# Weights of 1 and three second-read tiles in the batch-norm sums, and edge codes in 16 transfers, in a ragged-attention kernel

## The chip, the cores and the metric

The kernel runs on one core of one Trainium2 chip. The time is device microseconds of one execution. The time before is 331.27 us, the median of 4 runs from 331.06 to 331.68. A separate profiled execution gave the trace; its own time was 331.13 us, of which 326.7 us are the span of the profile.

## The reference

16384 rows of 256 features belong to 8 segments by `bids`, whose values come unsorted. Each row is to be found by its segment and its position (its number less the segment's start, which a binary search on the unsorted ids gives), so that several rows can fall on one place: one of them owns the place, the others lose it and read back the owner's row. Places before 0 or from LMAX on are at the segment's edges. Inside each segment there is softmax attention of all owners with each other, then a linear map, a batch norm over all 16384 rows, a relu and the residual.

```python
q = feat @ Wq                      # 256 -> 32, k likewise; v = feat @ Wv, 256 -> 256
starts = jnp.searchsorted(bids, jnp.arange(B, dtype=bids.dtype))
pos = jnp.arange(N, dtype=bids.dtype) - starts[bids]
qp, kp, vp = (pad(q), pad(k), pad(v))            # (8, 3072, .) by (bids, pos)
attn = jax.nn.softmax(masked qp kp^T, axis=-1)
r = (attn @ vp)[bids, pos]
t = r @ Wt
tn = (t - t.mean(axis=0)) / jnp.sqrt(t.var(axis=0) + EPS) * gamma + beta
return feat + jax.nn.relu(tn)
```

What matters here is the mean and the variance of `t`: sums over all 16384 rows of `t` and of its square, although `t` is computed only for the owners. An owner's row stands in the sums as often as it is read.

## The kernel before, in words

**Tiles.** The owners of a segment fill up to 6 tiles of 128 rows (`FT`), the rows that lost their place up to 3 more tiles for the whole kernel (`LT`); most other rows of the input read an edge row of one of the segments. The list of a segment's rows (`list_ahead`, L1147, `list_rows`, L1167) is made by VectorE (DVE) and TensorE (PE); GpSimd (POOL) then gathers the rows into `xs`. PE transposes them, projects q and k, and computes scores; ScalarE (ACT) takes exponents (`pa`, `pb`); `attend` (L1265) multiplies with the values, where the weights `Wv` and `Wt` are already joined, so that `scale` (L1278) has rows of `t` in `tk`. SyncE (SP) stores these to `t_rows` in DRAM.

**The sums.** For each tile of owners `square` (L1292) squares the rows on ACT, and `moments` (L1316) adds them and their squares to `acc` by two `scalar_tensor_tensor` on DVE, each row weighted by `reads_r`, the number of times it is read. `gather_reads` (L1191) fetches `reads_r` from DRAM, a tile of 128 weights at a time: 48 indirect gathers on POOL's queue. It is called in segments 1 to 6, where `list_part` and the slots of side work stand in the same hand-written order. `past(e)` (L1667) takes a few squares and moments from the lists `lag` and `squared`, so that they stay behind the attention by some steps.

**The order of the work.** The eight segments are one unrolled loop; in segment e the steps of `attend` are interleaved with the list, the gathers and the projection of later ones. The order in the source is the order of each engine's queue; semaphore waits are added from the tiles that instructions read and write. `slot()` puts in one or more pieces of side work (`work`): places of the losers, counts at the edges (`side_count`, which makes `below` and `above` from `pos`), `fill_rows` (L1633: clears `acc`, `xl`, `tl`, `ecat` and `reads_r`), and `part` (L1492).

**Edge codes.** Rows that read an edge row get it by a one-hot matmul in the last stage. `edge_of` in DRAM holds a code for each such row; `part` copies it into `eb` by 64 transfers on SP's queue, each to 16 partitions (L1503), and DVE compares it with the partition's own code and writes `hot`. In segment 1 POOL sets both `eb` buffers to 99 first (L1697), since the transfers leave 64 of the 128 partitions unwritten.

**The last segment** (L1714 on) takes its steps in the order 0, 1, 4, 5, 2, 3. SP starts ten loads of 1 MB of `feat` there. POOL computes `sel`, the selection of the edge rows, in six operations, and gathers the edge rows of the first seven segments into `ecat` (L1726). PE adds the last segment's, DVE joins them, ACT squares, and PE sums `ecat` weighted by `we` and `acc` into `sums`. Then come two 32x32 transposes, `scale`, `shift` and `y3`, the finished edge rows. After that a loop over 16 groups of 1024 rows adds `hot` times `y3` to the input rows (PE, then DVE's add into `f`), finishes the owners (`normal`, L1879, `normal_more`, both DVE), stores the groups (SP), and POOL scatters the owners (L1972) and the losers (L1985). The losers' rows, `tl`, are gathered from `t_rows` by the list `ridl` after the last segment (L1826). Ahead of the last segment come `slot(99)` and the memset of `none` on POOL (L1816, L1817).

Most operations are recorded by helpers, whose lines the profile shows: L802 matmul, L807 transpose, L812 activation, L817 and L818 copies on ACT and DVE, L821 tensor_tensor, L830 tensor_scalar (`ts`), L841 scalar_tensor_tensor, L854 reciprocal, L857 transposes on DVE, L860 memset, L877 gather, L893 scatter.

Of the kernel before, what the change touches and what calls it, by code (L numbers as in the profile page):

```python
# [14 lines left out]
AF = mybir.ActivationFunctionType  # L15
ALU = mybir.AluOpType
# [4 lines left out]
P = 128  # L21
NB = 8
# [6 lines left out]
FT = 6  # L29
FW = FT * P  # L30
LT = 3
# [869 lines left out]
def fast_path(nc, feat, bids, wq, wk, wv, wt, gamma, beta, out, bad):  # L901
    N, D = feat.shape
# [5 lines left out]
    NG = J // GT  # L908
    NL = NB + 1
    TT = NB * FT  # L910
    QA, QB = 4 * P, 2 * P
    pg = Fast(nc)

    room = ExitStack()
    start = nc._sbuf_addr_for_side("left")
# [23 lines left out]
    tk = new("tk", [P, TT, D])  # L939
# [126 lines left out]
    regs = pg.sized  # L1066

    def load(eng, key, ap, hi, lo=0):
        def emit(e):
            regs[key] = e.value_load(ap, min_val=lo, max_val=hi)  # L1070

        pg.op(eng, emit, [ap], [], bare=True)
# [36 lines left out]
    pg.tt(sm[:], sm[:], sc_[:], ALU.subtract, eng="POOL")  # L1109
    pg.tt(sm[:], sm[:], sa[:], ALU.add, eng="POOL")  # L1110

    def zero_fill(e):
        rows = xs[:, e * FT : (e + 1) * FT, :].rearrange("p t d -> p (t d)")
        pg.copy("ACT", rows, zero[:].to_broadcast([P, FT * D]))
# [32 lines left out]
    def list_ahead(e):  # L1147
        T = FT if e < NB else LT
        pg.ts(ge[:, 0, 0 : T * P], it16[:, 0 : T * P], cbeg[:, e : e + 1], ALU.is_ge)
        pg.ts(ge[:, 1, 0 : T * P], it16[:, 0 : T * P], cend[:, e : e + 1], ALU.is_ge, -1.0, ALU.mult)  # L1150
        pg.ts(pad[:, 0:T], rcol[:, 0:T], n_bc[:, e : e + 1], ALU.is_ge, float(N), ALU.mult)
        if e < NB:
            m = slice(e * FT, e * FT + T)
            pg.ts(mask[:, m], rcol[:, 0:T], n_1[:, e : e + 1], ALU.is_ge, NEG, ALU.mult)

    def list_sums(e, h, ps=None):
        ps = nb() if ps is None else ps
# [33 lines left out]
    def gather_reads(e):  # L1191
        for t in range(FT):
            m = e * FT + t
            pg.gather(reads_r[:, m : m + 1], reads_of, idx[:, m : m + 1], N)
# [95 lines left out]
    squared = []  # L1290

    def square(e, u):  # L1292
        n = e * FT + u
        x = sq[turn[1] % (4 if e < NB - 1 else 3)]
        turn[1] += 1
        pg.act(x[:], tk[:, n, :], AF.Square)
        return n, x
    def own_of(e):
        pg.ts(own1[:], b_f[:], float(e), ALU.is_equal)
        pg.stt(own1[:], tok[:], st_lo[:, e : e + 1], own1[:], ALU.is_ge, ALU.mult)  # L1300
# [13 lines left out]

    pg.copy("POOL", bs_f[:], bs_i[:])
    def moments():  # L1316
        m, s = squared.pop(0)
        x = m - TT + FT - 2
        one = rw[:, x : x + 1] if x in (0, 1) else reads_r[:, m : m + 1]
        pg.stt(acc[:, 0, :], tk[:, m, :], one, acc[:, 0, :], ALU.mult, ALU.add)  # L1320
        pg.stt(acc[:, 1, :], s[:], one, acc[:, 1, :], ALU.mult, ALU.add)

    cast_bids()
    pg.ts(own0[:], b_f[:], 0.0, ALU.is_equal, pm[:], ALU.mult)
# [80 lines left out]
    def slot(n=1):  # L1405
        for _ in range(n):
            if work:
                work.pop(0)()
# [34 lines left out]
    def edges():  # L1443
# [48 lines left out]
        def part(c):  # L1492
            x = eb[c % 2]

            def go():
                for k in range(C):
                    for r in range(4):
                        dst = x[32 * r : 32 * r + 2 * NB, k * W : (k + 1) * W]

                        def emit(e, c=c, k=k, r=r, dst=dst):  # L1500
                            g = regs[("order", C * c + k)]
                            src = edge_of[ds(g * W + r * NG * W, W)]
                            return e.dma_start(dst, src.unsqueeze(0).to_broadcast([2 * NB, W]))  # L1503

                        pg.op("SP", emit, [edge_of], [dst], dma=True)

            def end():
                pg.ts(
                    hot[:, C * c : C * c + C, :, :],
                    x[:].rearrange("e (k p u) -> e k u p", k=C, u=2), emod[:], ALU.is_equal,  # L1510
                )

            return go, end
# [114 lines left out]
    def fill_rows():  # L1628
        def zeros(x):
            f = x[:].rearrange("p t d -> p (t d)")  # L1630
            pg.copy("ACT", f, zero[:].to_broadcast([P, f.shape[1]]))

        def a():  # L1633
            zeros(acc)
            pg.set("DVE", ridl[:], NB * FW)
            pg.set("DVE", reads_r[:], 0.0)
            pg.tr32(gb[:].rearrange("p s i -> p (s i)"), graw[:].rearrange("p s i -> p (s i)"))

        def b():
            zeros(xl)  # L1640

        def c():
            zeros(tl)
            zeros(ecat)

        return [a, b, c]

    sums = ps_s[1]

    def by_row(w, m, x):  # L1650
        pg.mm(sums[:, 0:D], w[:], tk[:, m, :], start=False, stop=False)
        pg.mm(sums[:, D : 2 * D], w[:], x[:], start=False, stop=False)

    work.extend(places())
# [12 lines left out]
    def past(e):  # L1667
        n = (0, 0, 1, 1, 2, 2, 1, 1)[e]
        if past_e[0] != e:
            past_e[:] = [e, 0]  # L1670
        e_ = (e - 5) * FT + past_e[1]
        past_e[1] += 1
        if 0 <= e_ < NB:
            load("DVE", ("td", e_), arm[0:1, e_ : e_ + 1], 2)
        for _ in range(n):
            if squared:
                moments()
        for _ in range(n):
            if lag:
                squared.append(square(*lag.pop(0)))  # L1680
# [12 lines left out]
    for e in range(NB):  # L1693
        last = e == NB - 1
        n = e + 1
        if e == 1:
            for x in eb:  # L1697
                pg.set("POOL", x[:], 99.0)
            one, two, three_ = edges()
            sides = [*side_count(0, below[:]), *side_count(1, above[:])]  # L1700
            fills = fill_rows()
            work.extend([fills[0], *one, fills[1], two, *sides, fills[2], *three_, lambda: own_of(NB - 1)])
# [11 lines left out]
        if last:  # L1714
            for u in (0, 1, 4, 5, 2, 3):
# [10 lines left out]
                    pg.gather(ecat[:, 0, :], t_rows[0 : (NB - 1) * FW, :], eidx[:], (NB - 1) * FW)  # L1726
                if u == 4:
                    late[3]()
                if u == 5:
                    first = square(e, 1)  # L1730
                    for g in range(EARLY, MID):
                        load_group(g)
                if u == 1:
                    pg.act(row_sum[:], ones[:], AF.Identity, scale=reads_r[:, e * FT + 1 : e * FT + 2])
                if u == 3:
                    any_ = hot[0 : 2 * NB, 0:2, :, :].rearrange("p k u x -> p (k u x)")
                    pg.mm(sums[:], none[0 : 2 * NB, :], any_, start=True, stop=False)
                    by_row(row_sum, *first)
                if u == 3:
                    while lag:  # L1740
                        squared.append(square(*lag.pop(0)))
                    while squared:
                        moments()
                else:
                    past(e)
                if u == 2:
# [8 lines left out]
        else:  # L1755
# [18 lines left out]
            step(e, 2, lambda: project(n, 1))  # L1774
            if busy:
                list_part(e + 2, 1)
            if e == 1:
                gather_reads(0)
            if 1 <= e < 5:
                gather_reads(e)  # L1780
            past(e)
            slot(1 if busy else 2)
            if e + 3 < NB:
# [6 lines left out]
                own_of(e + 3)  # L1790
            if not busy:
                slot(2)
            if e >= 4:
                gather_reads(e + 1)
            if e == 3:
                losers()[0]()
# [17 lines left out]
        pg.end_region()  # L1814
        if e == NB - 2:
            slot(99)  # L1816
            pg.set("POOL", none[:], 0.0)  # L1817
    for e_ in range(NB + 1):
        load("POOL", ("g", e_), upto[0:1, e_ : e_ + 1], NG, 1)
# [148 lines left out]
    for e in range(NB):  # L1968
# [4 lines left out]
        for t in range(4, FT):  # L1973
            m = e * FT + t

            def emit(x, e=e, t=t, m=m):
                with x.If(regs[("t", e)] > t - 4):
                    x.wait_ge(row_done[e], 3 * (t - 3))
                    pg.put_now(x, out, idx[:, m : m + 1], tk[:, m, :], N)
# [61 lines left out]
```

## Time and profile before

| what | value |
|---|---|
| median of 4 runs | 331.27 us (331.06 to 331.68) |
| the profiled execution, its own time | 331.13 us |
| its span | 326.7 us |
| mean granted PE clock | 0.842 |
| gathers of `xs`, 48 on POOL | 50.7 us, 1057 ns each |
| gathers of `reads_r`, 48 on POOL | 51.1 us, 1064 ns each; 2.5 us to landing |
| copies of `edge_of` to `eb`, 64 on SP | 8.0 KB each, 1.6 us to landing |
| `acc` from `tk` and `reads_r`, 45 on DVE | 21.4 us, 476 ns each |
| `f` loads, 16 on SP | 1024 KB each, 11.0 us to landing |

A group's line gives its busy time, the mean of one instruction, and the idle time of the engine just before, with what ended it. A timeline line gives start, duration, engine, line of the kernel (often a helper's), operation and tiles, and in brackets how long the engine was idle before and what it waited for. The chain lists the work that ended last, followed back from the end, start and duration first. Busy time of an engine costs only where the chain runs through it.

### The profile page before, as it was taken

What the parts mean: (1) busy time and instruction counts of PE and PEld (TensorE: products, weight loads), DVE (VectorE), ACT (ScalarE), POOL (GpSimd) and SP (SyncE); (2) the same over time, 40 slices, a digit from 0 to 9 for tenths busy, and PEclk for the clock granted to TensorE, in tenths of its full rate; (3) what the DMA queues carried; (4) which work ended last, traced back from release to release, by engine and by line L of the source; (5) the groups of instructions that cost most, each with busy time, mean ns of one, the idle gap of its engine ahead of it and who ended that gap; (6) DMA issues with size and microseconds to landing.
All of it is one profiled execution on the core that took longest, in us unless ns stands there. A gap on an engine that the chain in (4) does not pass through costs nothing.

```text
span 326.7 us, 5094 instructions
## 1 busy us (share of the span) xinstructions
PE 255.9 (78%) x1407; PEld 168.2 (51%) x1407; DVE 236.3 (72%) x753; ACT 149.7 (46%) x291; POOL 173.7 (53%) x178
## 2 busy tenths in 40 slices
PE   5699799798998999899989999892868966465200
PEld 1566566475676677667866776581333422122100
DVE  4835679888668576659577898973489999999600
ACT  3127959485865584356547639792211311110000
POOL 6434318047778237614675476871040658787770
PEclk9559989799999999999999999998676965555555
DMA  3101104114022312311210121199999999997980
GB/s 102 34 23 36 31 2 134 42 49 139 7 61 57 102 34 69 96 47 39 83 34 2 51 83 32 59 307 416 401 409 392 313 422 424 421 414 277 393 305 2
DMA packets 22479, 51.83 MB, mean 159 GB/s; under 512 B 7502, under 2 KB 15776, under 8 KB 18474
## 3 DMA queue, kind: packets, MB, share of 16 engines
q1 hardware_dynamic: 15610, 40.85, 33.3%
q0 software_dynamic: 6288, 10.01, 9.9%
q10 hardware_dynamic: 544, 0.52, 0.5%
q8 instruction: 16, 0.26, 0.3%
q14 instruction: 21, 0.17, 0.2%
HBM read 25.37 MB, written 28.74 MB: 166 GB/s over the span
## 4 chain that ended last, share of the span: by engine, by line
PE 50%; DVE 21%; ACT 8%; issue 8%; POOL 6%; DMA 2%; POOLq 1%; DVEq 0%
PE ps L802 48%; DVE tk L821 4%; DVE f L821 4%; POOL out L893 3%; ACT pa L812 3%; PE ps L807 2%; ACT xT L812 2%; DMA ecat<-t_rows,eidx 2%; ACT vs L817 2%; DVE junk L828 1%; DVE k L818 1%; DVE tk L1897 1%; DVE tk L1899 1%; DVE w L821 1%; DVE acc L841 1%
## 5 line engine op out<-in xcount | busy, mean ns | idle before, releaser
L877 POOL DMA_INDIRECT xs<-in_r_feat,idx x48 | 50.7, 1057 | 78.1 <-DVE idx L841 29.0
L802 PE MATMUL ps<-vs,pa 128*128 128x257 f32 x312 | 78.1, 396 | 7.2 <-ACT vs L817 3.8
L802 PEld LDWEIGHTS ps<-vs,pa 128*128 128x128 f32 x312 | 57.9, 193 | 20.4 <-issue 7.0
L877 POOL DMA_INDIRECT reads_r<-reads_of,idx x48 | 51.1, 1064 | 14.6 <-issue 14.3
L893 POOL DMA_INDIRECT out<-tk,idx x32 | 38.4, 1200 | 25.7 <-DVE f L821 13.6
L802 PE MATMUL ps<-wvt,xT 128*128 128x256 f32 x156 | 37.4, 386 | 0.7 <-ACT vs L817 0.7
L802 PE MATMUL ps<-y,hot 16*128 16x256 bf16 x384 | 21.1, 369 | 21.4 <-DVE f L821 18.6
L817 ACT COPY f<-ps 128x1024 f32<-128x1024 f32 (+1 forms) x12 | 10.0, 834 | 57.7 <-PE ps L802 57.7
L812 ACT ACTIVATE pa<-ps,mask 128x512 f32<-128x512 f32 x48 | 29.5, 689 | 12.1 <-PE ps L802 12.1
L802 PEld LDWEIGHTS ps<-wvt,xT 128*128 128x128 f32 x156 | 28.8, 190 | 11.0 <-ACT sq L812 2.3
L802 PEld LDWEIGHTS ps<-y,hot 16*128 16x128 bf16 x384 | 11.3, 120 | 40.0 <-DVE f L821 30.5
L802 PE MATMUL ps<-f,ident 128*128 128x512 f32 x38 | 27.7, 854 | 1.8 <-DVE ecat L821 1.0
L821 DVE TENSOR_TENSOR f<-f,ps 128x1024 f32<-128x1024 f32 (+3 forms) x17 | 26.1, 1560 | 0.7 <-PE ps L802 0.7
L818 DVE COPY k<-ps 32x128 f32<-32x128 f32 x48 | 14.1, 294 | 16.7 <-PE ps L802 15.9
L812 ACT ACTIVATE xT<-ps,negx 128x512 f32<-128x512 f32 (+1 forms) x32 | 17.0, 582 | 18.9 <-PE ps L807 9.8
L817 ACT COPY vs<-ps 128x512 f32<-128x512 f32 x24 | 14.2, 593 | 19.0 <-PE ps L802 19.0
L812 ACT ACTIVATE q<-ps,cqk 96x512 f32<-96x512 f32 (+3 forms) x32 | 18.3, 573 | 9.9 <-PE ps L802 9.5
L841 DVE SCALAR_TENSOR_TENSOR acc<-tk,reads_r,acc 128x256 f32<-128x256 f32 x45 | 21.4, 476 | 1.6 <-issue 1.3
L802 PE MATMUL ps<-xT,w 128*128 128x512 f32 (+1 forms) x48 | 22.0, 585 | 0.0
L841 DVE SCALAR_TENSOR_TENSOR acc<-sq,reads_r,acc 128x256 f32<-128x256 f32 x45 | 21.7, 483 | 0.0
L854 DVE RECIPROCAL rdens<-ps 128x1 f32<-128x1 f32 x48 | 7.7, 161 | 19.2 <-PE ps L802 19.1
L812 ACT ACTIVATE pb<-ps,mask 128x256 f32<-128x256 f32 x48 | 19.4, 486 | 4.1 <-PE ps L802 3.8
(261 smaller groups left out, 422.8 us busy)
## 6 DMA issues: line engine op xcount, KB each, us to landing
f<-in_r_feat SPq DMA_DIRECT2D x16, 1024.0 KB, 11.0
out<-f SPq DMA_DIRECT2D x15, 1024.0 KB, 7.5
t_rows<-tk SPq DMA_DIRECT2D x8, 512.0 KB, 3.3
t_rows<-tk SPq DMA_DIRECT2D x8, 256.0 KB, 2.6
eb<-edge_of SPq DMA_DIRECT2D x64, 8.0 KB, 1.6
out<-f SPq DMA_DIRECT2D x2, 512.0 KB, 4.4
xs<-in_r_feat,idx POOLq DMA_INDIRECT x48, 2.8
reads_r<-reads_of,idx POOLq DMA_INDIRECT x48, 2.5
```

The source lines that it names most:

```text
L802: "PE", lambda e: e.matmul(out, lhsT, rhs, start=start, stop=stop, skip_group_check=True),
L807: return self.op("PE", lambda e: e.transpose(out, in_, ident), [in_, ident], [out], pred=pred)
L812: "ACT", lambda e: e.activation(out, in_, func, bias=bias, scale=scale), [in_, *more], [out]
L817: return self.op("ACT", lambda e: e.copy(out, in_), [in_], [out])
L818: return self.op(eng, lambda e: e.tensor_copy(out, in_), [in_], [out])
L821: return self.op(eng, lambda e: e.tensor_tensor(out, a, b, op), [a, b], [out])
L828: lambda e: e.tensor_scalar(out, a, s1, s2, op0, op1, accum_out=accum)
L841: else e.scalar_tensor_tensor(out, a, s, b, op0, op1),
L854: return self.op("DVE", lambda e: e.reciprocal(out, in_), [in_], [out])
L877: lambda e: e.indirect_dma_start(out=out, out_offset=None, in_=table, in_offset=bass.IndirectOffsetOnAxis(ap=ind, axis=0), bounds_check=n ...
L893: lambda e: e.indirect_dma_start(out=table, out_offset=bass.IndirectOffsetOnAxis(ap=ind, axis=0), in_=src, in_offset=None, bounds_check=n ...
L1897: v.tensor_tensor(y, y, scale, ALU.mult).then_inc(sem, 1)
```

## The change

`EARLY_B` is 6, the number of segments treated in a new way. There are three parts.

1. For segments 0 to 5 the weights in `reads_r` no longer come from DRAM. `list_ahead` sets a weight to 1 where the tile has a row and 0 where it has none. Segments 6 and 7 keep their 12 gathers, at the place L1794 in segments 5 and 6.
2. Rows of segments 0 to 5 that are read a second time are the losers' reads. Three gathers at the end of segment 6 fetch them from `t_rows` into `tl`, on POOL ahead of the memset of `none`. In the last segment they are put first in `lag`, with weight 1, for squares and moments like any other tile; `past` takes two of them at a time there, and the loop at step 3 alternates squares and moments. The gathers of `tl` at L1826 stay.
3. `edge_of` goes to `eb` in 16 transfers to all 128 partitions, each partition of a group of 32 reading the same 256 codes; the two memsets of `eb` go.

```diff
+    EARLY_B = NB - 2
...
         if e < NB:
             m = slice(e * FT, e * FT + T)
             pg.ts(mask[:, m], rcol[:, 0:T], n_1[:, e : e + 1], ALU.is_ge, NEG, ALU.mult)
+        if e < EARLY_B:
+            pg.ts(reads_r[:, m], rcol[:, 0:T], n_bc[:, e : e + 1], ALU.is_lt)
...
     def square(e, u):
-        n = e * FT + u
         x = sq[turn[1] % (4 if e < NB - 1 else 3)]
         turn[1] += 1
-        pg.act(x[:], tk[:, n, :], AF.Square)
-        return n, x
+        if e == NB:
+            row, w = tl[:, u, :], ones[:, 0:1]
+        else:
+            n = e * FT + u
+            i = n - TT + FT - 2
+            row, w = tk[:, n, :], rw[:, i : i + 1] if i in (0, 1) else reads_r[:, n : n + 1]
+        pg.act(x[:], row, AF.Square)
+        return row, w, x
...
     def moments():
-        m, s = squared.pop(0)
-        x = m - TT + FT - 2
-        one = rw[:, x : x + 1] if x in (0, 1) else reads_r[:, m : m + 1]
-        pg.stt(acc[:, 0, :], tk[:, m, :], one, acc[:, 0, :], ALU.mult, ALU.add)
-        pg.stt(acc[:, 1, :], s[:], one, acc[:, 1, :], ALU.mult, ALU.add)
+        row, w, s = squared.pop(0)
+        pg.stt(acc[:, 0, :], row, w, acc[:, 0, :], ALU.mult, ALU.add)
+        pg.stt(acc[:, 1, :], s[:], w, acc[:, 1, :], ALU.mult, ALU.add)
...
             def go():
                 for k in range(C):
-                    for r in range(4):
-                        dst = x[32 * r : 32 * r + 2 * NB, k * W : (k + 1) * W]
-
-                        def emit(e, c=c, k=k, r=r, dst=dst):
-                            g = regs[("order", C * c + k)]
-                            src = edge_of[ds(g * W + r * NG * W, W)]
-                            return e.dma_start(dst, src.unsqueeze(0).to_broadcast([2 * NB, W]))
-
-                        pg.op("SP", emit, [edge_of], [dst], dma=True)
+                    dst = x[:, k * W : (k + 1) * W]
+
+                    def emit(e, c=c, k=k, dst=dst):
+                        g = regs[("order", C * c + k)]
+                        src = edge_of.rearrange("(r w) -> r w", r=4)[:, ds(g * W, W)]
+                        return e.dma_start(dst, src.unsqueeze(1).to_broadcast([4, P // 4, W]))
+
+                    pg.op("SP", emit, [edge_of], [dst], dma=True)
...
-            pg.set("DVE", reads_r[:], 0.0)
+            pg.set("DVE", reads_r[:, EARLY_B * FT : TT], 0.0)
...
+        if e == NB - 1:
+            for _ in range(2 if lag and lag[0][0] == NB or len(lag) > 1 else 1):
+                if squared:
+                    moments()
+                if lag:
+                    squared.append(square(*lag.pop(0)))
+            return
...
         if e == 1:
-            for x in eb:
-                pg.set("POOL", x[:], 99.0)
...
+                if u == 0:
+                    lag[:0] = [(NB, t) for t in range(LT)]
...
-                    while lag:
-                        squared.append(square(*lag.pop(0)))
-                    while squared:
-                        moments()
+                    while lag or squared:
+                        if lag and len(squared) < 2:
+                            squared.append(square(*lag.pop(0)))
+                        else:
+                            moments()
...
-            if e == 1:
-                gather_reads(0)
-            if 1 <= e < 5:
-                gather_reads(e)
...
-            if e >= 4:
+            if EARLY_B <= e + 1:
                 gather_reads(e + 1)
...
         if e == NB - 2:
             slot(99)
+            for t in range(LT):
+                pg.gather(tl[:, t, :], t_rows[0 : EARLY_B * FW, :], ridl[:, t : t + 1], EARLY_B * FW)
             pg.set("POOL", none[:], 0.0)
```

## The prediction

> **What bounds the kernel now.** I read the page first (busy shares, the chain that ended last), then the timelines of DVE, PE and POOL around the places that the diff touches, then the chain of waits between them. The page:
>
> ```profile
> span 326.7 us, 5094 instructions
> PE 255.9 (78%) x1407; PEld 168.2 (51%) x1407; DVE 236.3 (72%) x753; ACT 149.7 (46%) x291; POOL 173.7 (53%) x178
> PE 50%; DVE 21%; ACT 8%; issue 8%; POOL 6%; DMA 2%; POOLq 1%; DVEq 0%
> ```
>
> There are three regimes. From about 60 to 212 us TensorE sets the pace: the chain is 76% matmuls there, and all waits of PE between 63 and 212 us come to 7.3 us. From 212 to 240 us it is a chain through the last segment's sums (edge, `sel`, gather of `ecat`, sums, `y3`). After 240.9 us VectorE works nearly without a gap (36.11 of the 37.00 us from 257 to 294). Whatever isn't on one of these three costs nothing now. The 48 gathers of `reads_r`, which are what the diff mainly removes, are POOL's (51.1 us in the page's group); no PE wait longer than 0.2 us in 63 to 212 us ends on anything but ACT, and none on POOL or a gather. So they are off the path.
>
> **Part 1: weights by VectorE instead of 36 gathers.** Removed: 36 POOL gathers of 1.00 us, each 0.30 us after the one before, so 47 us of POOL's queue, for which only later POOL gathers of `xs` waited. Those are early: the ones issued from 92.20 us write tiles that the PE transposes read at 107.6 us, with a landing of 2.1 to 4.2 us. Gain 0. Added: six `ts` of 128x6, one for each segment 0 to 5, in `list_ahead`. Such a `pad` or `mask` starts 0.13 us after the last (61.40, 61.53), so +0.13 each. Only that of segment 0 (8.4 us, in a DVE chain that PE waits for) is on the path: **+0.13**. The others lie beside PE; the one of segment 2 matters in part 2.
>
> **Part 2: the edge codes.** 64 transfers of 8 KB become 16 of 64 KB on SP's queue, the same 16 source rows now written to all 128 partitions. Bytes written rise from 0.5 to 1 MB, 0.5 MB at times when the DMA engines are 0 to 30% busy, and SP issues fewer. `hot` is built from them in the middle segments, long after the 1.6 us landing of one. Nothing. But the two POOL memsets of `eb` that filled the unwritten partitions go, and these are on the path. POOL, DVE and PE, from their timelines:
>
> ```profile
> 55.49 1.87 POOL L860 MEMSET eb<- 128x1024 bf16 x2
> ```
>
> ```profile
> 55.55 1.89 DVE L830 TENSOR_SCALAR below<-pos 128x128 f32<-128x128 f32 x1
> 55.70 1.81 DVE L830 TENSOR_SCALAR above<-pos 128x128 f32<-128x128 f32 x1
> 57.43 0.21 DVE L830 TENSOR_SCALAR at<-pos 128x128 f32<-128x128 f32 x1
> ...
> 58.41 0.48 DVE L830 TENSOR_SCALAR tk<-ps,rdens 128x256 f32<-128x256 f32 x1
> ```
>
> ```profile
> 59.04 3.06 PE L802 MATMUL ps<-vs,pa 128*128 128x257 f32 x8 [1.72 <-DVE tk L830]
> 61.89 0.64 PE L807 MATMUL ps<-ident,xs 128*128 128x128 f32 x2
> 62.32 2.31 PE L802 MATMUL ps<-xT,w 128*128 128x512 f32 x4
> ```
>
> The same `ts` of 128x128 takes 0.21 us at 57.43 and 1.8 to 1.9 us while the memset runs (55.49 to 57.36); both finish as it finishes. `at` would start at 55.70 + 0.15 = 55.85 instead of 57.43: **1.58 us** lost, and everything behind it on DVE is back to back until `tk` at 58.41, for which PE stood 1.72 us (59.04). So the stall's 1.58 us are regained at PE, which would then wait 0.14.
>
> What is late next: the stretches by granted clock (us, busy time and instructions of PE, PEld, DVE, ACT, POOL, then clock, DMA share, GB/s):
>
> ```profile
> 56.35:59.76 3.41, 1.58 (x9) 1.21 (x10) 3.24 (x11) 1.38 (x3) 1.01 (x2) 1.00 0.00 0
> 59.76:63.17 3.41, 3.41 (x9) 2.32 (x8) 3.20 (x20) 1.93 (x5) 0.00 (x0) 0.50 0.25 82
> ...
> 209.95:213.36 3.41, 1.83 (x9) 1.29 (x9) 3.12 (x10) 3.41 (x9) 2.71 (x3) 1.00 0.58 190
> ```
>
> After the stretch with PE busy 1.58 us the clock is 0.50 for 3.41 us. After the one with 1.83 us busy (209.95) it stays 1.00. Without the stall the first stretch would have PE busy some 3 us, so I take it that the half-clock stretch goes. Then the eight attend matmuls take 1.97 us (the group at 53.92) and not 3.06, the transposes lose 0.2 and the projection 0.4: another 1.7 us of PE. DVE allows less. It runs without a gap from 57.43 to 63.44, and the `k` copy that follows (64.67 now, waiting 1.22 us for PE) can't start before 63.44 - 1.58 + 0.13 (the new `ts` of segment 2) = 61.99. So all behind that copy moves from 64.67 to 62.0: 2.67 us earlier. With the +0.13 of part 1, **-2.54 us** at the start of the stretch that PE bounds, and PE hands it on to 212 us. If the clock stayed at half, the gain would be the stall alone, 1.58 - 0.13 = 1.45.
>
> The Trainium skill ("TensorE: Matmul & The Clock Gate", What's actually happening, and its table under Why this matters for your kernels) speaks against the second half: the clock falls back after at least one whole idle window of about 3.4 us, and gaps under some 3 us are safe. By it a gap of 1.72 us is not the cause, the half-clock stretch would come anyway, and the sum would be by 1.1 us worse. The row shows half clock after a gap of 1.72 us; I go by the row.
>
> **Part 3: three tiles more in the last segment.** Three gathers of `tl` are put into POOL's queue after the last `reads_r` gather, ahead of the memset of `none`, the six `sel` and the gather of `ecat`. POOL's timeline there:
>
> ```profile
> 212.64 1.00 POOL L877 DMA_INDIRECT reads_r<-reads_of,idx  x1 [0.30 <-issue]
> 213.63 0.22 POOL L860 MEMSET none<- 128x128 bf16 x1
> 214.95 5.47 POOL L830 TENSOR_SCALAR sel<-edge,rcol 128x128 f32<-128x128 f32 x6 [1.10 <-DVE edge L821]
> 220.70 1.10 POOL L877 DMA_INDIRECT ecat<-t_rows,eidx  x1 [0.27 <-issue]
> 239.11 1.13 POOL L877 DMA_INDIRECT tl<-t_rows,ridl  x1 [0.30 <-issue]
> ```
>
> Their data (segments 0 to 5, `ridl` since 206 us) are ready, so they cost POOL time only: three times 1.13 + 0.30 = 4.29 us. Of this, 1.10 us is the slack in which POOL waited for `edge`. So `sel` starts 3.19 us later against its inputs. The `sel` then lie beside fewer DVE instructions of the `we` work (0.72 to 0.99 us each now): -0.25. The gather of `ecat` lands 6.56 us after its issue, DVE adds it at 227.28, and between them the chain has nothing else:
>
> ```profile
> 220.70 6.56 DMA ecat<-t_rows,eidx
> 227.28 0.43 DVE ecat L821
> 227.73 0.42 ACT ecat L812
> 228.20 5.79 PE ps L802 x8
> ```
>
> I keep 6.56, since the DMA engines are 95 to 101% busy with ten 1 MB loads before and after. This part costs **+2.93 us**. Bounds: if the landing is 4.4 (the least of the three `tl` gathers, under the same loads), 2.2 less, +0.8; if gathers take the 1.74 us of the slowest `reads_r` and the landing 6.9 (its slowest), +5.1.
>
> The work on these tiles: three squares on ACT (0.42 us) and six `acc` (0.48 us, or 0.39 in a row). They stand at the head of the list in the last segment, so ACT waits at the first square, with the segment's second `tk` scaling behind it, and DVE waits at the moments with the reciprocals behind them; PE's next attends and thus all of the segment wait. The first gather is issued at about 213.9, lands 4.4 to 6.4 us later, by 220; the second by 222. ACT now has all but done by 222 us and PE has nothing at all from 223.60 to 227.00, so some 4 us of cover, and with `ecat` 2.9 us later, 7. The late part is DVE: one more pair of `acc` comes after the `ecat` add than now (three pairs and not two), 0.9 us: the last now ends at 229.60, then at 230.5 against 230.2 + 2.9 for the sum that reads it. 0 by this count; without that cover, up to +0.9. Nothing replaces the final gathers of `tl`; they stay.
>
> **Tail.** From `y3` on all is as before, 3 tiles of 128x256 apart (0.39 MB, 0.95 us of DMA at 410 GB/s). By the table of stretches DVE is busy 15.93 of 16.10 us (240.90 to 257) and 36.11 of 37 (to 294) at DMA shares of 0.97 and 1.01, so the end shifts with `y3`: 0.
>
> **Sum** -2.54 + 2.93 = **+0.39**. The profiled execution took 331.13 us (span 326.7 and 4.4 around it): 331.5. The median of the four runs shown is 331.27, 0.14 above: 331.66. I forecast **331.6**.
>
> **Rivals.**
> - *Slower: the half clock stays.* The stretch of 59.76 comes without the 1.72 us gap too (1.83 us of busy PE in the stretch at 209.95 kept the full clock, 1.58 at 56.35 did not). It decides if PE's busy time in the stretch ahead stays below some 1.6 to 1.8 us. Gain 1.45 in place of 2.54: 331.27 - 1.45 + 2.93 = 332.75, **332.7**, slower.
> - *Faster: DMA sets the tail, or the gather lands sooner.* For it: the DMA shares of the tail, as full as DVE. The loads of the last segment hang on SP and on PE's progress, not on `ecat`, so they start 2.54 us earlier; with 0.95 us more bytes, -1.6: 331.27 - 1.6 = **329.7**. A landing of 4.4 gives 331.66 - 2.2 = 329.5 by another way. Against it: after 240.9 us DVE too has no gaps, and DVE starts with `y3`.
> - *The memset is not what stretches the two `ts`.* Both then stay at 1.8 us, no gain: 331.27 + 0.13 + 2.93 = **334.3**. Against it: the ends agree to 0.15 us, and the same form takes 0.21 right after.
>
> **Chances.** Forecast case 0.40, half clock 0.22, DMA tail or short landing 0.25, no stall gain 0.08, other 0.05 (a wait of DVE or ACT on `tl` that reaches the sums). Two runs of this kernel can be told apart from about 0.2%, 0.66 us: the bounds are 330.6 and 331.9. The forecast case, with its unknown half a microsecond, is 0.28 within, 0.03 below, 0.09 above. Faster then has 0.28 (0.25 and 0.03), slower 0.41 (0.22 + 0.08 + 0.09 and most of the rest), same 0.31. Range: down to the DMA case, 329.6; up to the half-clock case and 0.3 over it, 333.0; outside are the 0.08, part of the rest and the far ends of the landing. Cases of both signs hold much, so the likeliest one's own range: 331.0 to 332.2.
>
> **What would show it.** `below` and `above` take 0.2 us each near 55.5, the attend's wait before 59 us is gone, the clock reads 1.00 from 56 to 66, the `k` copy starts at 62.0 (part 2 right). 12 gathers of `reads_r` and 6 of `tl`; `sel` starts at about 215.6 (218.1 - 2.54), `ecat` is gathered at 221.1 and added at 227.7 (part 3). DVE's first add of `f`, 240.93 now, at 241.3. I am wrong if `sel` still waits for `edge`, if the `ecat` landing is far from 6.6, or if the end moves by another amount than that first add.

## The result, and the profile after

The changed kernel took 330.43 us (median of 44 runs, 323.75 to 332.74), the kernel before 331.64 (70 runs, 327.54 to 333.52): 1.2 us less. The ratio is given as 0.9837 (0.9807 to 0.9868), since of the changed kernel only the executions within 1.5% of its fastest count there, four of the 44; the medians alone give 0.9964. The profiled execution took 329.43 us, 1.7 under the one before. In the experiments below, on other chips, the same two kernels stand up to 35 us apart.

The page of the changed kernel:

```profile
span 325.0 us, 4870 instructions
PE 253.3 (78%) x1407; PEld 167.7 (52%) x1407; DVE 237.3 (73%) x765; ACT 150.6 (46%) x294; POOL 136.1 (42%) x143
PE 46%; DVE 20%; issue 11%; POOL 9%; ACT 7%; DMA 3%; POOLq 1%; DVEq 0%; SPq 0%
```

POOL is busy 38 us less, the span is 1.7 us shorter, and POOL's share of the chain rose from 6 to 9%: the 36 gathers were off the path, and POOL's queue ahead of `sel` is now on it (`reads_r` and `tl`, 2 and 1%). The timelines of DVE and PE where the memsets were:

```profile
55.75 0.23 DVE L830 TENSOR_SCALAR below<-pos 128x128 f32<-128x128 f32 x1
55.90 0.22 DVE L830 TENSOR_SCALAR above<-pos 128x128 f32<-128x128 f32 x1
...
62.21 1.22 DVE L818 COPY k<-ps 32x128 f32<-32x128 f32 x4
```

```profile
57.68 1.98 PE L802 MATMUL ps<-vs,pa 128*128 128x257 f32 x8 [0.17 <-DVE tk L830]
59.50 0.38 PE L807 MATMUL ps<-ident,xs 128*128 128x128 f32 x2
```

The two `ts` take 0.23 us and not 1.9, PE's wait went from 1.72 to 0.17, its eight matmuls from 3.06 to 1.98, and the `k` copy from 64.67 to 62.21. On the way into the last segment, ACT's scaling of `tk` that stood at 207.74 is at 205.22: 2.52 us earlier. POOL's queue ahead of `sel`, and the chain behind it:

```profile
210.12 1.00 POOL L877 DMA_INDIRECT reads_r<-reads_of,idx  x1 [0.30 <-issue]
211.43 0.99 POOL L877 DMA_INDIRECT tl<-t_rows,ridl  x1 [0.30 <-issue]
212.72 1.26 POOL L877 DMA_INDIRECT tl<-t_rows,ridl  x1 [0.30 <-issue]
214.28 1.00 POOL L877 DMA_INDIRECT tl<-t_rows,ridl  x1 [0.30 <-issue]
...
215.60 5.04 POOL L830 TENSOR_SCALAR sel<-edge,rcol 128x128 f32<-128x128 f32 x6
220.91 1.10 POOL L877 DMA_INDIRECT ecat<-t_rows,eidx  x1 [0.27 <-issue]
```

```profile
220.91 6.41 DMA ecat<-t_rows,eidx
...
229.33 0.89 DVE acc L841 x2
230.26 3.33 PE ps L802 x6
```

`sel` has no idle time before it: it waits for the queue and no longer for `edge`. `ecat` is added at 227.34, 0.06 us later than before, so 2.58 of the 2.52 us gained are given back. The sums (230.26, 3.33 us) now wait for the last pair of `acc`. DVE's first add of `f` is at 240.53, 0.40 us earlier than before.

The end moved by more, 1.77 us. POOL's scatters set it. In both traces 38 of them follow each other without a pause but the 0.30 us of issue, once a store has landed, and the span ends 9.23 us after the start of the last. The first of them and the VectorE pair beside it, before (two fences) and after (two fences):

```profile
264.54 1.92 POOL L893 DMA_INDIRECT out<-tk,idx  x1 [4.12 <-SPq L1908]
266.76 0.98 POOL L893 DMA_INDIRECT out<-tk,idx  x1 [0.30 <-issue]
```

```profile
264.38 2.48 DVE L821 TENSOR_TENSOR tk<-tk,ss 128x1024 f32<-128x1024 f32 x2
```

```profile
263.87 0.98 POOL L893 DMA_INDIRECT out<-tk,idx  x1 [3.85 <-SPq L1921]
```

```profile
263.99 2.48 DVE L821 TENSOR_TENSOR tk<-tk,ss 128x1024 f32<-128x1024 f32 x2
```

A scatter that starts inside the pair takes up to 1.92 us; one that has started 0.12 us ahead of it takes 0.98. In the 38 there are six that took over 1.4 us before and five after; from the first start to the last it is 52.98 us before (264.54 to 317.52), 51.88 after (263.87 to 315.75). So the 1.77 are 0.67 of earlier start and 1.10 of a shorter run. Of the run, 0.94 is the missed pair; of the later scatters one is 0.36 shorter (1.56 for 1.92) and one 0.21 longer.

A second trace of the changed kernel (from chip 5 below, where the kernel before has the same median as here; there is no second trace of before without the delay that the experiments show) separates what recurs from what doesn't:

| us | before | changed | changed, second trace |
|---|---|---|---|
| start of `sel` | 214.95 | 215.60 | 215.67 |
| landing of the `ecat` gather | 6.56 | 6.41 | 7.14 |
| `ecat` added by DVE | 227.28 | 227.34 | 228.06 |
| DVE's first add of `f` | 240.93 | 240.53 | 241.46 |
| first scatter starts | 264.54 | 263.87 | 264.89 |
| last scatter starts | 317.52 | 315.75 | 316.76 |
| first to last scatter | 52.98 | 51.88 | 51.87 |

The shorter run is there again, the earlier start is not: the first add differs by 0.93 us between two executions of the same kernel, more than the whole forecast. The first scatter starts 23.61 us after the first add of `f` before, 23.34 and 23.43 after, and the VectorE pair 23.45 or 23.46 in all three. Whether the scatter misses the pair is a matter of some 0.2 us (0.16 into it before, 0.12 and 0.03 ahead of it after), which nothing in the change was meant to move; so the missed pair may be luck, and it is not shown to follow from the change.

### The profile page after: what moved, and what is told of

The parts are those of the page before. It is cut to its first block, busy times and chain, and to the rows that moved or that the text cites. A ratio compares the mean times of both kernels' runs of the same rounds, so it can differ in the third digit from the quotient of the medians.

```text
span 325.0 us, 4870 instructions
## 1 busy us (share of the span) xinstructions
PE 253.3 (78%) x1407; PEld 167.7 (52%) x1407; DVE 237.3 (73%) x765; ACT 150.6 (46%) x294; POOL 136.1 (42%) x143
## 4 chain that ended last, share of the span: by engine, by line
PE 46%; DVE 20%; issue 11%; POOL 9%; ACT 7%; DMA 3%; POOLq 1%; DVEq 0%; SPq 0%
PE ps L802 44%; DVE tk L821 4%; DVE f L821 4%; POOL out L893 3%; ACT xT L812 2%; DVE acc L841 2%; ACT pa L812 2%; PE ps L807 2%; DMA ecat<-t_rows,eidx 2%; POOL reads_r L877 2%; ACT vs L817 1%; DVE junk L828 1%; POOL tl L877 1%; DVE tk L1910 1%; DVE tk L1912 1%
## 5 line engine op out<-in xcount | busy, mean ns | idle before, releaser
L893 POOL DMA_INDIRECT out<-tk,idx x32 | 36.4, 1137 | 26.7 <-DVE f L821 14.3
L802 PE MATMUL ps<-y,hot 16*128 16x256 bf16 x384 | 19.9, 354 | 23.1 <-DVE f L821 20.6
L812 ACT ACTIVATE q<-ps,cqk 96x512 f32<-96x512 f32 (+3 forms) x32 | 18.3, 573 | 10.4 <-PE ps L802 10.1
L802 PE MATMUL ps<-q,k 32*128 32x512 f32 (+1 forms) x124 | 20.0, 560 | 0.0
```

The lines of the kernel that those rows point to most:

```text
L802: "PE", lambda e: e.matmul(out, lhsT, rhs, start=start, stop=stop, skip_group_check=True),
L812: "ACT", lambda e: e.activation(out, in_, func, bias=bias, scale=scale), [in_, *more], [out]
L893: lambda e: e.indirect_dma_start(out=table, out_offset=bass.IndirectOffsetOnAxis(ap=ind, axis=0), in_=src, in_offset=None, bounds_check=n ...
```

## The experiments

The runs were made in five sets, each on one chip, beside the kernel before. In four of the five (chips 7, 2, 13, 11) the kernel before took 365 to 375 us in the median, in the fifth (chip 5) 331.69, like the first runs. So the parts are read within a set. Each chip has one set, so a property of the chip and one of the occasion can't be told apart.

**Chip 7.** Before: 375.00 (11 runs). The changed kernel itself:

> The changed kernel itself, for its trace and its spread. Theory A (the two traces so far): 2.5 us are gained before 60 us, 2.6 are given back ahead of the ecat gather, and the end is set by GpSimd's run of row scatters, which starts when a store of a group has landed; then this run is again about 1.2 us under the kernel before (330.4 against 331.6), and its executions spread by more than a us with the phase of the clock stretches. Rival B (some executions near 324 us are its true time and the rest are disturbed): most executions here are near 324.

It took 340.36 us (6 runs), ratio 0.9131 (0.9081 to 0.9182). Neither theory had a difference of 34.6 us.

Part 2 alone:

```diff
-            for x in eb:
-                pg.set("POOL", x[:], 99.0)
...
+                    dst = x[:, k * W : (k + 1) * W]
```

> The kernel before with part 2 alone: 16 transfers for the edge codes and no memsets of eb. Theory A: the two tensor_scalar at 55.5 us take 0.2 us each, PE's wait of 1.72 us goes, the half-clock stretch at 59.76 goes or moves, and everything from 62 us to the edge rows is 2.6 us earlier; nothing is given back, so the first add of f comes 2.6 us earlier (238.3) and the time is about 2.5 us under before (329.1). Rival C (the stall is hidden by a later wait): edge rows and the end as before, 331.6. Rival D (the end hangs on DMA and not on y3): first add earlier by 2.6, end by under 1.

It took 367.50, ratio 0.9836 (0.9770 to 0.9902): 7.5 us less and not 2.5. `below` and `above` are short (0.23 us) as theory A has it; the rest is not explained by it.

Only the memsets, put back into the changed kernel:

```diff
         if e == 1:
+            for x in eb:
+                pg.set("POOL", x[:], 99.0)
```

> The changed kernel with the two GpSimd memsets of eb put back where they were; parts 1 and 3 and the 16 transfers stay. Theory A: the stall is back, everything behind it about 2.5 us later than in the changed kernel, some 332.9. Rival E (the gain comes from the 36 fewer gathers): as the changed kernel, 330.4, and below is short again.

344.55 against 340.36, 4.2 us longer, and `below` took 1.90 us at 55.22 again. That the memsets on GpSimd stretch the two `ts` is shown; for these 4.2 us rival E falls. The 4.2 us rest on six runs of each, which don't overlap (343.69 to 347.02 and 338.47 to 343.09). The two traces can't show what they consist of: they stand 4.4 us apart already ahead of the memsets (`below` at 55.22 and at 50.81).

The weights of segments 6 and 7 a segment earlier:

```diff
-            if EARLY_B <= e + 1:
-                gather_reads(e + 1)
+            if EARLY_B <= e + 2 < NB:
+                gather_reads(e + 2)
```

> The changed kernel, but the weights of segments 6 and 7 are gathered one segment earlier, where GpSimd's queue is idle (158 to 178 us). Theory A: GpSimd's queue is what delays sel (it works without a gap from 189 to 215.6 us); now sel starts when edge is there, about 212.4 instead of 215.6, the squares of tl no longer hold up ACT for 4.5 us, the ecat gather is issued some 3.2 us earlier and the first add of f comes 2.5 to 3.2 us earlier, with an end of 327.5 to 328. Rival F (the ecat gather lands when the loads let it): ecat lands at about 227 all the same, and the time is that of the changed kernel.

339.49, 0.9 us less than the changed kernel, within the spread here. It is taken up again on chip 5 below.

**Chip 2.** Before: 365.46 (11 runs).

> The kernel before with part 2 alone (16 transfers for the edge codes, no memsets of eb), once more beside the other parts: in the run p2_only all kernels stood at far longer times (before 375.0 us), with engines idle for up to 11 us while GpSimd worked through its gathers of reads_r. Theory A: if before is near 331 here, the first add of f is 2.6 us earlier (238.3) and the time about 329.1. Rival C (stall hidden by a later wait): 331.6. Rival G (the gathers of reads_r themselves hold up other engines, on some chips): before near 375 again, and this some 6 us less.

357.35, ratio 0.9780 (0.9719 to 0.9840). Rival G is nearest, though it expected a kernel before near 375 us and 6 us less, and 8.1 were found.

Part 1 alone:

```diff
+        if e < EARLY_B:
+            pg.ts(reads_r[:, m], rcol[:, 0:T], n_bc[:, e : e + 1], ALU.is_lt)
...
-            if e == 1:
-                gather_reads(0)
-            if 1 <= e < 5:
-                gather_reads(e)
```

> The kernel before with part 1 alone: weights of segments 0 to 5 are set by VectorE, 36 gathers of reads_r fewer. What it leaves out: rows read a second time are missing from the sums. Theory A: off the path, +0.1 us, so the time of before (331.6 where before is there). Rival E (the gathers cost time): 1 us or more under before. Rival G: where before is near 375, this is near 345, since then the gathers are the difference.

337.75, ratio 0.9266 (0.9214 to 0.9318): 27.7 us less for 36 gathers, 0.77 each on average. Theory A's "off the path" is wrong here.

Parts 1 and 2 without part 3:

```diff
-            for t in range(LT):
-                pg.gather(tl[:, t, :], t_rows[0 : EARLY_B * FW, :], ridl[:, t : t + 1], EARLY_B * FW)
...
-                if u == 0:
-                    lag[:0] = [(NB, t) for t in range(LT)]
```

> The changed kernel without part 3: no early gathers of tl, no squares and moments of them. What it leaves out: rows read a second time are missing from the sums. Theory A: sel starts when edge is there, 2.5 us ahead of before (212.4), the ecat gather some 3 us earlier than in the changed kernel, first add of f at about 238 against 240.5, the time 2 to 2.6 us under the changed kernel (328). Rival F (ecat lands when the loads let it): as the changed kernel, 330.4.

334.55; `sel` waits for `edge` again (4.61 us), as theory A says. The first add of `f` is at 242.82, so the rest of that theory (238, and 328 in all) is not met. The changed kernel was not run in this set.

> The changed kernel with the weights of segments 6 and 7 gathered one segment earlier, beside the parts (in the run early_reads it was 0.9 us under the changed kernel, 339.49 against 340.36, with before at 375.0). Theory A: sel at 212.4 and not 215.6, no wait of ACT for tl, first add of f 2.5 to 3 us earlier than in the changed kernel, time near 328. Rival F: as the changed kernel, 330.4. Rival H (the tail's scatters and stores end when DMA lets them): first add 3 us earlier, time by less than 1 us.

333.16, though it has the three gathers that no_tl leaves out: the gain of the earlier weights at the least covers what these three cost. The first add of `f` is at 244.73 in its trace.

**Chip 13.** Before: 372.67 (11 runs), and a trace of it:

> The kernel before, for a trace of it under the conditions of these experiments (365 to 375 us, where the first four runs stood at 331.27). Theory K (a run of indirect transfers back to back on GpSimd's queue holds back PE's signals to the other engines): ACT and VectorE show waits of several us for a PE that had long finished, in the stretches of the reads_r gathers (75 to 90, 137 to 146, 176 to 192, 214 to 237 us), that end when the run of gathers ends; PE is not slower by itself. Rival N (a slower chip in general): every stretch is longer by the same share.

377.83. Its timelines of PE, ACT and POOL (three fences):

```profile
76.33 1.03 PE L802 MATMUL ps<-vs,pa 128*128 128x257 f32 x4
83.11 1.23 PE L802 MATMUL ps<-vs,pa 128*128 128x257 f32 x2 [5.75 <-issue]
95.65 2.08 PE L802 MATMUL ps<-vs,pa 128*128 128x257 f32 x4 [11.31 <-ACT vs L817]
```

```profile
82.48 0.59 ACT L817 COPY vs<-ps 128x512 f32<-128x512 f32 x1 [6.98 <-remote]
93.86 1.26 ACT L812 ACTIVATE pa<-ps,mask 128x512 f32<-128x512 f32 x2 [10.79 <-remote]
```

```profile
75.98 1.11 POOL L877 DMA_INDIRECT reads_r<-reads_of,idx  x1 [0.31 <-issue]
...
90.47 1.00 POOL L877 DMA_INDIRECT reads_r<-reads_of,idx  x1 [0.30 <-issue]
```

"remote" is a release that the profile puts on no instruction of this core. The scores that `pa` reads had left PE by 75.4 us; ACT starts at 93.86, 2.4 us after POOL's last gather. The trace of the first chip has no such wait there (`pa` at 77.33). In the tail it is the same with the scatters (DVE, then PE, then POOL):

```profile
364.44 2.29 DVE L821 TENSOR_TENSOR f<-f,ps 128x2048 f32<-128x2048 f32 x1 [12.47 <-remote]
```

```profile
346.98 1.47 PE L802 MATMUL ps<-y,hot 16*128 16x256 bf16 x24 [0.73 <-DVE f L821]
```

```profile
360.94 0.98 POOL L893 DMA_INDIRECT out<-tl,idx  x1 [0.30 <-issue]
```

PE's last matmuls end at 348.45, DVE adds them at 364.44, 2.5 us after the end of the last scatter. Compared instruction by instruction with the first trace, PE falls behind in the stretches with gathers and is level between them, so it is not a slower chip (rival N falls). How far it falls behind goes with the number of gathers that POOL issues back to back:

| gathers in the run | starts of the runs (us) | PE falls behind by (us) |
|---|---|---|
| 3 | 164.5, 179.7, 217.7 | 0 |
| 6 | 11.9, 28.4, 47.4 | 0 |
| 9 | 224.1, 239.7 | 3.3, 3.5 |
| 12 | 108.7, 143.0 | 6.5, 4.6 |
| 15 | 185.9 | 7.4 |
| 18 | 68.0 | 18.4 |

In the run of 18, the first delay comes at its seventh gather (75.98, the first POOL line above). So in this trace a run of six is free and the price lies in the longer ones; runs of `xs` and of `reads_r` that touch count as one. The runs differ in what PE has to do beside them too, so the table is no price list.

> The changed kernel on the chip of this call. Theory K: some 30 us under before if before is near 365 to 375, some 1.2 us under it if before is near 331. Rival B: near 324.

340.98 (6 runs).

Shorter runs of gathers:

```diff
             if busy:
                 list_part(e + 2, 0)
+            if e == 1:
+                gather_reads(0, range(3))
+            if 1 <= e < 5:
+                gather_reads(e, range(3))
```

> The kernel before, with the gathers of reads_r in threes: three after the first half of a segment's xs gathers and three after the second half (six and six in segment 1), so that runs of 12 to 18 transfers back to back become runs of 6 to 9. Theory K (the length of the run decides): well under before, by 8 us or more. Theory L (each gather of single values costs by itself): as before, within 3 us.

387.84, 15.2 us more. The first gathers now stand ahead of the clearing of `reads_r`, so that part of the weights is lost, and DVE's memset of it waits 13.57 us for them (81.31). Without that it would be some 1.6 us over before; the gain of 8 us or more that shorter runs should have had isn't there. But the edit didn't shorten the runs: in its trace the later ones have 9, 9, 12, 12, 18, 9 and 9 gathers, and PE again falls behind by 13.7 us in the run of 18 (from 184.4) and by 3.5, 6.0 and 10.4 in runs of 9, 12 and 12. It is a miss in its design, and says nothing against the length of the run as the cause. No run here changed the length alone.

Gathers of whole rows in their place:

```diff
+            pg.gather(f8[:, m % GT, :], feat, idx[:, m : m + 1], N, track=False)
```

> The kernel before with part 1, and in the place of the 36 gathers of reads_r 36 gathers of 128 rows of 1 KB into a tile that nothing reads; rows read a second time are missing from the sums. Theory K: as long as before, since the number of transfers and their places are the same. Theory L (transfers of 4 bytes do it): as p1_alone, some 28 us under before.

374.56, 1.9 us over before, while they replace gathers whose absence gave 27.7 us on chip 2. Size doesn't matter (theory L falls); in the run of 18 PE falls behind by 18.3 us again.

**Chip 11.** Before: 375.13 (11 runs). Other work in the place of the 36 gathers, on SP's queue and on GpSimd:

```diff
+            pg.dma("SP", f8[:, m % GT, 0:1], reads_of[m * P : (m + 1) * P, :])
```

> The kernel before with part 1, and in the place of the 36 gathers of reads_r 36 transfers of 128 values of 4 bytes that SP's queue issues into a tile that nothing reads; rows read a second time are missing from the sums. Theory K (what GpSimd issues holds up the others): as p1_alone, which was 28 us under before. Rival O (the small transfers themselves do it, whoever issues them): as before.

```diff
+            pg.iota(f8[:, 0:2, :].rearrange("p t d -> p (t d)").bitcast(F16), [[1, 1024]], 0)
```

> The kernel before with part 1, and in the place of the 36 gathers of reads_r 36 iota instructions of some 1 us each on GpSimd into a tile that nothing reads; rows read a second time are missing from the sums. Theory K in its narrow form (it takes indirect transfers): as p1_alone, 28 us under before. Rival P (a busy GpSimd is enough): as before.

342.41, ratio 0.9249 (0.9059 to 0.9439), and 341.67, ratio 0.9221 (0.9065 to 0.9377): 33 us under before, both. Neither the small transfers nor a busy GpSimd does it; it takes indirect transfers that GpSimd issues. What a direct transfer issued by GpSimd would cost was not tried, so the indirect kind and the queue that it goes through are not separated.

A pause in the scatters:

```diff
-    look("POOL")
+    look("POOL", [added])
```

> The changed kernel, where GpSimd waits for VectorE's last add of f before the last three scatters (those of the losers). Theory K: in the changed kernel of these experiments PE issues the last hot matmuls one by one, 0.7 to 1.7 us apart, as long as GpSimd scatters, and the last adds of f start only some 2 us after the last scatter; now they start some 2 us after the last scatter ahead of the wait, 4 us earlier, and the three scatters come after them; the time within 3 us of the changed kernel. Rival Q (PE's last matmuls wait for the loads or for code): the adds start as late as before, and the time is some 8 us longer.

343.06 (changed kernel 340.90). Its DVE and POOL:

```profile
323.05 2.29 DVE L821 TENSOR_TENSOR f<-f,ps 128x2048 f32<-128x2048 f32 x1 [6.91 <-remote]
```

```profile
319.98 0.99 POOL L893 DMA_INDIRECT out<-tk,idx  x1 [0.30 <-issue]
326.30 0.99 POOL L893 DMA_INDIRECT out<-tl,idx  x1 [5.33 <-SPq L1921]
```

The add comes 2.1 us after the scatter ahead of the pause, as theory K has it; rival Q falls. Ending the scatters earlier frees PE's signal; it gains no time, since the three scatters come after. Without the pause, in the trace of the changed kernel of this chip, the last scatter ends at 320.99 and the add comes at 323.42, 2.4 us after.

> The changed kernel beside these. Theory K: 30 to 35 us under before if before is at 365 to 375; near 330.4 if before is near 331.6, and then the three kernels above show no difference of more than 2 us among them and p1_alone.

340.90, ratio 0.9120 (0.8754 to 0.9487).

**Chip 5.** Before: 331.69 (17 runs, 329.98 to 333.13).

> The weights of segments 6 and 7 gathered one segment earlier, as a pair with the changed kernel on one chip; so far 339.49 against 340.36 (chip of the first call). Theory A with K: the number of indirect transfers is the same, sel starts when edge is there, and the time is 1 to 3 us under the changed kernel. Rival F: the same time.

> The changed kernel as the other half of that pair. Theory K: 32 us under before if before is at 365 to 378.

The changed kernel took 330.56 (12 runs, 325.16 to 332.61), ratio 0.9911 (0.9871 to 0.9951); with the early weights 328.48 (6 runs, 327.82 to 329.93), ratio to before 0.9924 (0.9897 to 0.9951). By the medians that is 1.1 and 3.2 us under before; the two ratios overlap, so that the early weights beat the changed kernel rests on the medians alone (on chip 7 too they were 0.9 us under it). POOL with the early weights:

```profile
207.15 1.00 POOL L877 DMA_INDIRECT tl<-t_rows,ridl  x1 [0.31 <-issue]
...
213.35 5.96 POOL L830 TENSOR_SCALAR sel<-edge,rcol 128x128 f32<-128x128 f32 x6 [4.99 <-DVE edge L821]
219.59 1.10 POOL L877 DMA_INDIRECT ecat<-t_rows,eidx  x1 [0.27 <-issue]
```

`sel` waits for `edge` and not for the queue; the squares of `tl` follow without a wait on ACT. `ecat` is gathered 1.3 us earlier than in the changed kernel (220.89 in its trace of this chip), the first add of `f` comes at 240.05 against 241.46. Theory A has the direction; `sel` beside more of DVE's work takes 5.96 us and not 4.95, and eats 1.0 of it.

## Why the prediction was wrong

It had +0.39 us (331.6); the profiled executions differ by -1.7, the medians by -1.2. The measured ratio lies below its range (329.6 to 333.0 us); it is made by the four quick executions, whose cause is open (last point), while the median of 330.43 lies inside. The steps below are about the -1.2.

- **Part 2, the memsets: right.** -2.54 was predicted, -2.52 measured on the way into the last segment; memsets_back shows what stretches the two `ts`. The `k` copy came at 62.21 for 61.99.
- **The half-clock stretch: right in the trace, its rule partly open.** The stretches of the changed kernel (us, busy time and instructions of PE, PEld, DVE, ACT, POOL, clock, DMA share, GB/s):

```profile
56.68:60.09 3.41, 3.19 (x17) 2.44 (x18) 3.24 (x19) 2.64 (x6) 0.00 (x0) 1.00 0.25 82
60.09:63.51 3.42, 3.35 (x17) 2.06 (x16) 3.20 (x14) 3.23 (x8) 0.00 (x0) 1.00 0.07 19
227.35:230.76 3.41, 1.62 (x3) 0.59 (x4) 3.34 (x13) 2.48 (x4) 0.00 (x0) 1.00 1.03 414
```

  With PE busy 3.19 of 3.41 us the next stretch keeps the full clock; after 1.62 the clock is at half from 230.76 to 234.17. That the memsets bring the half-clock stretch is well supported: all eight traces with them have one of 3.41 us that starts between 58.3 and 60.1, and of the twelve without them none has one between 43 and 70 us. The prediction's limit (some 1.6 to 1.8 us of busy PE) holds in the first two traces, but not beyond them. In the second trace of the changed kernel:

```profile
227.37:230.78 3.41, 2.17 (x6) 0.88 (x6) 2.72 (x8) 2.16 (x4) 0.00 (x0) 1.00 1.00 408
230.78:234.19 3.41, 3.22 (x6) 1.92 (x7) 0.68 (x6) 0.32 (x1) 0.00 (x0) 0.50 1.03 409
```

  Here half clock follows 2.17 us of busy PE, and in memsets_back full clock follows 1.56 (212.57 to 215.98). So PE's busy time in the stretch ahead doesn't decide it alone, and the rule stays open. The Trainium skill ("TensorE: Matmul & The Clock Gate", What's actually happening) lets the clock fall after at least one idle window of about 3.4 us; here it fell after stretches of 3.41 us in which PE was busy for 1.58 to 2.17 us, and the measurement decides.
- **Part 3: right in kind, a little too large.** `sel` 0.65 us later than before (215.60 against 214.95), as +3.19 - 2.54 had it. 2.58 and not 2.93 by the `ecat` add (its terms give 2.94): the six `sel` took 5.04 us for 5.47, the landing 6.41 for 6.56. In the second trace the landing is 7.14 and the `ecat` add 0.78 us later than before, so this term is known to some 0.7 us only. The added `acc` pair, put at 0 by the count and up to 0.9 without cover, is the sums' last wait (0.87 us in both traces), but in the first trace the clock makes up for it: the `we` matmuls start in a stretch at full clock, 1.12 us and not 2.07. From the `ecat` add to the first add of `f` it is 0.46 less than before there, which no term had. The first add was forecast at 241.3; it came at 240.53 and 241.46.
- **"Tail ... so the end shifts with `y3`: 0": wrong.** VectorE has no gaps there, but it is done 18 us before the end (the last add of `f` starts at 304.67 and ends at 306.96, span 325.0). POOL's 38 scatters, most of them 1.29 us apart, set the end. From the first to the last it is 52.98 us before and 51.88 and 51.87 in the two traces of the changed kernel (51.87 in early_reads_c too): 1.10 less, 0.94 of it by missing one VectorE pair. The prediction's own sign of being wrong came: the first add moved by -0.40 and the end by -1.77 (+0.53 and -0.76 in the second trace). The mean of the two ends, -1.27, is near the -1.2 of the medians; with one trace of before, and some 0.2 us deciding on which side of the pair the scatter falls, why it fell on the better side stays open; it may be luck. I read the tail off VectorE's busy share and not off the last instruction of the chain. The faster rival (DMA sets the tail) had nearly the time, but its mechanism isn't what the traces show: the run starts with a store's landing, and 51.9 to 53.0 us of scatters follow.
- **"36 POOL gathers ... Gain 0": wrong where the kernel before takes 365 to 375 us.** They cost 27.7 us on chip 2, and on chip 11 other work in their place 33 us less. What the trace of before could show, it showed (no PE wait on a gather); the price isn't in it. Shown is that there, long runs of indirect transfers issued by GpSimd hold back PE's signals to ACT and DVE, whatever the size of the rows (p1_alone, wide_rows, hw_reads, pool_busy, wait_add, and the table of before_again). Why it happens in some sets and not in others is open, and so is why part 2 is worth 7.5 to 8 us there.
- **Open: the few quick executions.** Four of the 56 executions of the changed kernel on the chips without that delay took 323.75 to 326.88 us. They are the four with a mean granted clock of 0.861 to 0.864, and no other lies there. No trace is of one of them, and what falls away in them was not seen. A guess from two other traces: in after_again and p2_only the half-clock stretch at the start lasts 10.24 us and not 17.07, no second one comes near 39 us, and `below` starts at 50.81 and 50.82 where all the others have it from 54.9 to 56.7. That is about the size of what the quick executions gain.

## What to carry to other kernels

Find the engine that issues the last instruction, and count its run to the end, before a busy share elsewhere is called the bound. A step that one engine is given is paid in that engine's queue: free the queue (move later-needed gathers into its idle time) before hanging new ones ahead of a critical one. And where a kernel can do without indirect gathers, leave them out even if one trace shows them off the path: on another chip or another occasion they may hold up the other engines. Where they are needed, short runs of them look safer than long ones (read off the traces; no run changed the length alone).

## What was not expected of the hardware

- On chip 2, 36 indirect gathers that GpSimd issued cost 27.7 us, 0.77 each on average. On chip 13 gathers of 1 KB rows cost as much as those of 4-byte values (374.56 and 372.67 us, the changed kernel 340.98); on chip 11 SP's transfers and GpSimd's iota in their place were 33 us under before. The price is not even: in the trace of before on chip 13 PE lost nothing beside runs of three and six, and 18.4 us beside a run of 18. In the first runs and on chip 5 the same gathers cost nothing that shows.
- While such a run lasts, PE's own instructions can come one at a time: late `hot` matmuls of the changed kernel on chip 13 started 0.7 to 2.1 us apart (316.01 to 325.16), where the last 24 took 1.47 us together.
- Two memsets of 128x1024 bf16 on GpSimd (1.87 us together) stretched a VectorE `ts` from 0.22 to 1.9 us, and a VectorE pair with two operands a GpSimd scatter from 0.98 to 1.92.
- From the start of the last scatter to the end of the span it is 9.23 us in four traces (before, the changed kernel, and the two of chip 5).
